# A hybrid attention and feed-forward kernel: reordered opening, paired exponentials, and a projection at another place in the first feed-forward pass

## The chip, the cores and the metric

The kernel runs on one core of one Trainium2 chip. The metric is the device time of one execution in microseconds (us). A core has five engines, each with its own queue of instructions: TensorE (PE, matrix products; its weight loads are shown apart as PEld), VectorE (DVE), ScalarE (ACT), GpSimd (POOL) and SyncE (SP, which here only issues transfers). They meet through semaphores. Each engine takes its own instructions in the order in which they were written into its queue, so an instruction that waits holds up everything behind it on its engine.

## The reference, cut to what matters

```python
x = x + attn_a(layernorm(x))   # windowed attention, 2 branches
x = x + ffn(layernorm(x))      # 4-bit weights, gelu(tanh)
x = x + attn_b(layernorm(x))   # causal attention, 16 heads, rotary
x = x + ffn(layernorm(x))      # the same weights again

# attn_a, per image, tokens of 16 channels
qkv  = tok @ qkv_w
attn = softmax(q * scale @ k.T)            # windows of 8 tokens
x1, x2 = attn @ v + depthwise_conv3x3(v)   # branch 0: rows, branch 1: columns
att  = concat(x1, x2) @ proj_w + proj_b
tok  = tok + layernorm(att) * ln_w + ln_b

# ffn
W = LUT[codes] * scales                    # gate, up (2048x256), down (256x2048)
out = (gelu(x @ Wg.T) * (x @ Wu.T)) @ Wd.T
```

`x` is 4 x 512 x 256 in f32; the four entries of the batch are called b = 0 to 3 here.

## The kernel before

**Stages.** The opening does the windowed attention of b = 0 alone, because no feed-forward work exists yet. Then come three stretches in which the feed-forward pass f0, f1, f2 of one b (`ffn`, lines 709 to 764) runs beside the window attention of the next b (`beside_window`, lines 1240 to 1260). After that the causal attentions run beside the passes f3, s0, s1, s2, and s3 ends the kernel alone.

**Order on the engines.** In the opening (lines 1158 to 1234) PE, DVE and ACT take their instructions in the order of the program text. After it only PE does (`weave`, lines 1078 to 1088). For the other engines a planner of the framework makes a fixed order at build time, by the order of the text and its own estimate of what is ready. `queue_behind` adds "not ahead of this instruction on the engine" to that.

**The weave.** The window work is a generator that yields a number of microseconds after each piece. `weave` sums these and, for each 0.86 us, puts one step of the feed-forward pass into PE's queue: one product of 512 columns or two of 256, 0.86 us of PE. A pass has 96 steps: four for the gate and up products of each of its 16 hidden blocks, and 32 for the down product, which comes in two halves after 8 blocks each. A larger yield thus puts more feed-forward products ahead of the next window piece on PE.

**The window attention.** `window_front` normalises over the group of 16 tokens: statistics, a product with `halves` (`pm`, line 249), a root on POOL (`inv_root`, lines 92 and 93), the scaling of `xa`, transposes (`yTp`), a copy `yT`, then products with the expanded weights `bw` and `taps` (`qkv`, `lepe`) whose results ACT copies into `T`. `window_consts` makes the expanded weights; it stops four times, and each `next(made)` runs it to its next stop. `window_parts` holds the pieces of the attention itself: `products` (the elementwise q times k, tile `tq`), `scores_piled` (sums on PE by products with the identity) or `scores_here` (sums on DVE), `peak` (maximum and subtraction), `power` (the exponential on ACT), `total_piled` or `total_here` (the sum of the exponentials, on PE or DVE), `shares` (the division), `weighted` (times v, tile `tv`), `values_piled` or `values_here` and `take_piled`. In the opening most sums are piled on PE; in the stretches all are on DVE. The tile `sc` of the scores has one buffer and `tmp`, which holds `tq` and `tv`, has two.

**The end of a window.** `window_back` gives four pieces: `project` (transposes `aTp`, copy, product with `pw`, then `pr` on DVE), `turn` (an inverse root and the tiles `z` on DVE), `move` (128 small products that bring `z` into the row layout, `zp`) and `add` (into `X`). `norm_rows` then makes the normalised transposed input `xT` of the feed-forward pass.

**The weights.** `dequant` expands the 4-bit weights in 12 words of six DVE instructions each, 72 items; `some(words, n)` runs n of them. Each word's two loads go to SP's queue. `along(middle, words, 6)` spends six items beside each piece of the first stretch's window and adds their yields.

**Unread products.** `busy(n)` issues n products whose result nobody reads, so that PE is not idle. All of them write one tile `idle`, which takes one of the three buffers of `fbank`; the others serve `sc`, `va`, `pg`, `pu` and `po`.

The planned lengths of the first stretch's middle:

```python
yield from between(scaled(middle, 0.87 if b == 1 else 1.22), other)
project, turn, move, add = window_back(a1, a2, wconst, b, state)
for hf in range(2):
    yield from scaled(project(hf), 0.0 if b == 1 else 1.0)
yield from turn()
```

Of the kernel before, what the change touches and what calls it, by code (L numbers as in the profile page):

```python
# [10 lines left out]
F32 = mybir.dt.float32  # L11
# [8 lines left out]
C = 16  # L20
# [15 lines left out]
def hybrid_kernel(  # L36
# [72 lines left out]
    def window_consts(aw):  # L109
        c = {}  # L110
        wrep = aw.tile([P, 48], F32, name="wrep")
        nc.gpsimd.dma_start(out=wrep, in_=qkv_w.unsqueeze(0).broadcast_to([8, C, 48]))
        prep = aw.tile([P, C], F32, name="prep")
        nc.gpsimd.dma_start(out=prep, in_=proj_w.unsqueeze(0).broadcast_to([8, C, C]))
        sh = aw.tile([P, 3, 8], F32, name="sh")
        nc.gpsimd.dma_start(out=sh, in_=shift)
        cw = aw.tile([P, 2, 3, 3, 8], F32, name="cw")
        for k, src in enumerate((conv_w0, conv_w1)):
            nc.gpsimd.dma_start(
                out=cw[:, k].rearrange("p a b c -> p (a b c)"), in_=src.broadcast_to([P, 72])  # L120
            )
        ones = aw.tile([C, P], F32, name="ones")
        nc.vector.memset(ones, 1.0)

# [114 lines left out]
    def window_front(a1, a2, c, b, y, state):  # L239
# [65 lines left out]
                    y[:, s, :], y[:, s, :], AF.Identity, bias=mean[:, s : s + 1], scale=rs[:, s : s + 1]  # L305
                )
        if b == 0:
            busy(4)
        yield 5.5 if b < 2 else 3.0

        ps = pair(f"yTp{b}")
# [29 lines left out]
        nc.scalar.copy(T[:, 7].rearrange("p s j d -> p (s j d)"), lp)  # L341
        state[b] = (y, T)

    def busy(n, cols=P):

        for _ in range(n):
            nc.tensor.matmul(idle[:, 0:cols], ident, idle_in[:, 0:cols], start=True, stop=True)

    def window_parts(a1, a2, c, b, state):

# [160 lines left out]
    def window_middle(a1, a2, c, b, state):  # L511

        w = window_parts(a1, a2, c, b, state)

        def late(br):

            behind = last_on(mybir.EngineType.Activation).name
            queue_behind(w["power"](br), behind)

        for br in range(2):  # L520
            for hf in range(2):
                ins = w["products"](br, hf)
                if br == 0:

                    queue_behind(ins, state[b - 1, "moved"] if hf == 0 else state[f"f{b - 1}"])
                w["scores_here"](br, hf)
                yield 4.6
                if br == 1 and hf == 1:
                    late(0)
            w["peak"](br)  # L530
            yield 1.4
        for br in range(2):
            w["total_here"](br)
            w["shares"](br)
            yield 2.3
            for hf in range(2):
                w["weighted"](br, hf)
                w["values_here"](br, hf)
                yield 5.1
                if br == 0 and hf == 0:  # L540
                    late(1)

    def window_back(a1, a2, c, b, state):

# [107 lines left out]
                yield 0.55  # L652


    def norm_rows(pool, b, name, out, first=4.5, at_once=False):

        xb = X[b]
        mv = pool.tile([P, 4, 2], F32, tag="mv", name=f"mv_{name}")
        def behind(ins):

            if at_once:
                queue_behind(ins, before)

        before = last_on(mybir.EngineType.DVE).name
        for i in range(4):
            st = pool.tile([P, 6], F32, tag="st", name=f"st_{name}_{i}")
            behind(nc.vector.bn_stats(st, xb[:, i, :]))
            nc.vector.bn_aggr(mv[:, i, :], st)
        rs = pool.tile([P, 4], F32, tag="rs", name=f"rs_{name}")
        inv_root(rs, mv[:, :, 1])  # L670
        xT = pool.tile([P, 2, 512], F32, tag="xT", name=f"xT_{name}", bufs=3)
        if at_once:
            yield 1.0
        before = last_on(mybir.EngineType.DVE).name
        ps = None if at_once else pair(f"xTp_{name}")
        xns = []
        for i in range(4):
            xn = pool.tile([P, 2, P], F32, tag="xn", name=f"xn_{name}_{i}", bufs=4)
            ins = nc.vector.tensor_scalar(
                xn,  # L680
                xb[:, i, :].rearrange("p (j par) -> p par j", par=2),
                mv[:, i, 0:1],
                rs[:, i : i + 1],
                ALU.subtract,
                ALU.mult,
            )
            behind(ins)
            state[name] = ins.ins.name
            xns.append(xn)
            if not at_once:  # L690
                yield first if i == 0 else 0.6
            elif i < 3:
                continue
            else:
                yield first
                ps = pair(f"xTp_{name}")
            for k in range(0 if at_once else i, i + 1):
                for par in range(2):
                    nc.tensor.transpose(ps[:, par, k * P : (k + 1) * P], xns[k][:, par, :], ident)
        nc.scalar.copy(xT, ps)  # L700
        out.append(xT)
        yield 1.3

# [437 lines left out]
    with ExitStack() as left:  # L1141
# [11 lines left out]
        idle = fbank.tile([P, 512], F32, tag="ps", name="idle")  # L1153
        idle_in = ident
        xa = window_load(a2, 0, nc.scalar)
        made = window_consts(aw)
        words = dequant(take, a1)
        with tc.manual_schedule(
            engines={mybir.EngineType.PE, mybir.EngineType.DVE, mybir.EngineType.Activation}
        ):  # L1160
            wconst = next(made)
            idle_in = wconst["sel"].rearrange("p q h n -> p (q h n)")
            front = window_front(a1, a2, wconst, 0, xa, state)
            some(front, 4)
            next(made)
            some(words, 9)
            rows_load(0)
            some(front, 3)
            ahead = window_front(a1, a2, wconst, 1, window_load(a2, 1), state)
            for b in range(1, B):  # L1170
                rows_load(b)
            drain(front)
            w = window_parts(a1, a2, wconst, 0, state)
            w["products"](0, 0)
            w["scores_piled"](0, 0)
            some(words, 3)
            next(made)
            next(ahead)
            w["products"](0, 1)
            w["scores_piled"](0, 1)  # L1180
            next(ahead)
            w["products"](1, 0)
            next(made)
            w["scores_piled"](1, 0)
            w["peak"](0)
            w["power"](0)
            next(ahead)
            w["total_piled"](0)
            w["products"](1, 1)
            w["scores_piled"](1, 1)  # L1190
            some(words, 3)
            w["shares"](0)
            w["weighted"](0, 0)
            next(ahead)
            w["values_piled"](0, 0)
            w["peak"](1)
            w["power"](1)
            w["total_piled"](1)
            w["weighted"](0, 1)
            w["values_piled"](0, 1)  # L1200
            next(ahead)
            rows_shift(wconst, 0)
            rows_shift(wconst, 1)
            some(words, 3)
            w["shares"](1)
            w["weighted"](1, 0)
            w["values_piled"](1, 0)
# [27 lines left out]

        after += [last_on(eng) for eng in (mybir.EngineType.DVE, mybir.EngineType.Activation)]
# [3 lines left out]
        def beside_window(b):  # L1240
# [136 lines left out]
```

## Time and profile before

| what | value |
|---|---|
| median of 4 runs | 1039.63 us (1038.51 to 1041.49) |
| the profiled execution: its own time | 1040.77 us |
| its span, first to last instruction | 1039.1 us |
| PE busy | 1008.8 us, 97% |
| DVE busy | 669.0 us, 64% |
| ACT busy | 357.5 us, 34% |
| POOL busy | 133.5 us, 13% |

The shares are means over stages that differ. The page of the profile also cuts the span into 40 slices of 26 us and gives the busy tenths of each engine in each. PE's busy time includes the unread products, and the ends of its products are modelled. The "granted clock" (PEclk) is the share of the full TensorE clock that the chip gave; a 0.50 means that products run at half speed.

Where the opening goes, from the instructions in order of time (us from the start of the span):

| event | start, us |
|---|---|
| first unread product (it waits for `sel` of POOL) | 6.31 |
| last statistic of b = 0 done | 7.84 |
| product `pm` | 9.71 |
| root on POOL, both instructions | 10.90 to 12.86 |
| expansion of the weights `bw` to `taps` on DVE | 14.39 to 16.67 |
| first `qkv` product | 16.72 |
| first `tq` product on DVE | 23.32 |
| `X` of b = 0 complete (`add`) | 76.08 to 77.30 |
| first product of the pass f0 | 86.56 |
| window of b = 1: `zp` | 178.46 |

### The profile page before, as it was taken

To read this page: it belongs to the slowest core of one execution; us is meant where nothing else is said; L and a number is where in the kernel's file an instruction comes from. 1 tells how busy PE (TensorE), PEld (TensorE's weight loads), DVE (VectorE), ACT (ScalarE), POOL (GpSimd) and SP (SyncE) were. 2 spreads that over 40 slices of the span, in tenths; PEclk is the share of its full clock that TensorE was granted. 3 is DMA by queue.
4 is the path that set the end of the run, shared out by engine and by line. 5 is a ranking of instruction groups with operands and counts; after the bars stand their busy time and mean duration, and the time that the engine had idled before them with its cause. 6 is when DMAs were issued, how large, how long until landed. Compare 5 with 4: busy or idle time off the path is not lost.

```text
span 1039.1 us, 13256 instructions
## 1 busy us (share of the span) xinstructions
PE 1008.8 (97%) x5058; PEld 587.2 (57%) x5058; DVE 669.0 (64%) x1579; ACT 357.5 (34%) x587; POOL 133.5 (13%) x265
## 2 busy tenths in 40 slices
PE   6999998999999999999999999999999999999998
PEld 4864545656566575564475554664644745446556
DVE  6889996956685777846586646666465576543111
ACT  2553432043213212435514435235254253451110
POOL 4100100000000012111240112310112301120000
PEclk8999999999999999999999999999999999999999
DMA  7201100000000020000000000000000000000000
GB/s 183 86 9 33 61 20 3 19 1 0 2 1 0 1 68 1 1 1 1 1 1 1 1 1 1 6 16 1 1 1 1 21 1 1 1 1 21 1 0 21
DMA packets 14031, 15.27 MB, mean 15 GB/s; under 512 B 2080, under 2 KB 10440, under 8 KB 13936
## 3 DMA queue, kind: packets, MB, share of 16 engines
q1 hardware_dynamic: 12416, 13.37, 4.3%
q10 hardware_dynamic: 1136, 0.92, 0.3%
q8 instruction: 40, 0.66, 0.3%
q0 software_dynamic: 416, 0.13, 0.2%
q14 instruction: 23, 0.19, 0.1%
HBM read 12.32 MB, written 2.10 MB: 14 GB/s over the span
## 4 chain that ended last, share of the span: by engine, by line
PE 79%; DVE 16%; issue 2%; POOL 1%; ACT 1%; POOLq 0%; DVEq 0%; ACTq 0%
PE pg_s L718 11%; PE pu_s L736 11%; PE po_s L753 10%; PE pg_f L718 7%; PE pu_f L736 7%; PE po_f L753 7%; PE s L904 4%; PE o L989 4%; PE sT L953 4%; PE qkv_b L843 3%; PE qkv L326 2%; DVE tq L398 1%; DVE tq L379 1%; DVE tq L390 1%; PE qkT L880 1%
## 5 line engine op out<-in xcount | busy, mean ns | idle before, releaser
L919 DVE CUSTOM_DVE_ANT_0 junk<-s,mask 128x512 f32<-128x512 f32 (+3 forms) x256 | 110.1, 487 | 36.8 <-PE s L904 19.8
L736 PE MATMUL pu_f<-xT_f,u 128*128 128x512 f32 x256 | 124.9, 603 | 3.0 <-ACT gs_f L730 2.0
L718 PE MATMUL pg_s<-xT_s,g 128*128 128x512 f32 x256 | 126.7, 603 | 0.0
L718 PE MATMUL pg_f<-xT_f,g 128*128 128x512 f32 x256 | 124.4, 600 | 2.2 <-ACT xT_f L700 1.1
L736 PE MATMUL pu_s<-xT_s,u 128*128 128x512 f32 x256 | 125.4, 601 | 0.0
L753 PE MATMUL po_f<-d,it_f 128*128 128x256 f32 x512 | 117.8, 381 | 1.4 <-DVE it_f L745 1.4
L753 PE MATMUL po_s<-d,it_s 128*128 128x256 f32 x512 | 118.0, 382 | 0.0
L753 PEld LDWEIGHTS po_s<-d,it_s 128*128 128x128 f32 x512 | 95.2, 190 | 20.8 <-issue 8.8
L753 PEld LDWEIGHTS po_f<-d,it_f 128*128 128x128 f32 x512 | 95.0, 190 | 19.8 <-issue 5.6
L969 POOL TENSOR_SCALAR_AFFINE_SELECT e<-e 128x256 f32<-128x256 f32 x128 | 52.7, 424 | 344.3 <-ACT e L965 341.4
L965 ACT ACTIVATE e<-sT 128x1024 f32<-128x1024 f32 (+1 forms) x72 | 66.5, 969 | 72.0 <-PE sT L953 72.0
L736 PEld LDWEIGHTS pu_f<-xT_f,u 128*128 128x128 f32 x256 | 46.9, 191 | 57.2 <-issue 49.3
L718 PEld LDWEIGHTS pg_f<-xT_f,g 128*128 128x128 f32 x256 | 46.9, 191 | 56.2 <-issue 45.6
L718 PEld LDWEIGHTS pg_s<-xT_s,g 128*128 128x128 f32 x256 | 45.9, 190 | 56.8 <-issue 50.9
L736 PEld LDWEIGHTS pu_s<-xT_s,u 128*128 128x128 f32 x256 | 46.1, 190 | 54.4 <-issue 50.2
L727 DVE SCALAR_TENSOR_TENSOR g_s<-g_s,gs_s 128x512 f32<-128x512 f32 x48 | 33.2, 691 | 58.7 <-ACT g_s L726 58.3
L730 ACT ACTIVATE gs_f<-pg_f 128x512 f32<-128x512 f32 x48 | 28.6, 596 | 93.0 <-PE pg_f L718 92.9
L745 DVE TENSOR_TENSOR it_f<-pu_f,gs_f 128x512 f32<-128x512 f32 x48 | 32.8, 683 | 32.2 <-PE pu_f L736 32.2
L724 ACT COPY gs_s<-pg_s 128x512 f32<-128x512 f32 x48 | 28.2, 587 | 67.7 <-PE pg_s L718 67.5
L904 PE MATMUL s<-kT,qT 16*128 16x384 f32 (+3 forms) x512 | 50.0, 467 | 0.0
L762 DVE TENSOR_TENSOR X<-po_s,X 128x256 f32<-128x256 f32 x32 | 13.5, 421 | 53.9 <-PE po_s L753 53.9
L989 PE MATMUL o<-e,V 128*32 128x256 f32 (+3 forms) x512 | 44.4, 441 | 0.4 <-PE sT L953 0.4
(224 smaller groups left out, 1361.7 us busy)
## 6 DMA issues: line engine op xcount, KB each, us to landing
X<-in_x_dram SPq DMA_DIRECT2D x4, 512.0 KB
out_dram<-X SPq DMA_DIRECT2D x16, 128.0 KB
xa<-in_x_dram SPq DMA_DIRECT2D x28, 64.0 KB
pkg<-in_gate_p_dram SPq DMA_DIRECT2D x4, 256.0 KB
sbg<-in_gate_s_dram SPq DMA_DIRECT2D x4, 256.0 KB
pku<-in_up_p_dram SPq DMA_DIRECT2D x4, 256.0 KB
sbu<-in_up_s_dram SPq DMA_DIRECT2D x4, 256.0 KB
pkd<-in_down_p_dram SPq DMA_DIRECT2D x4, 256.0 KB
```

What stands on the lines that cost most here:

```text
L718: nc.tensor.matmul(pg, Wf["g"][par][q][:, o : o + P], xT[:, par, :], start=par == 0, stop=par == 1)
L727: nc.vector.scalar_tensor_tensor(g2, g2, 1.0, gs, ALU.add, ALU.mult)
L736: nc.tensor.matmul(pu, Wf["u"][par][q][:, o : o + P], xT[:, par, :], start=par == 0, stop=par == 1)
L745: behind_due(nc.vector.tensor_tensor(it, pu, gs, ALU.mult))
L753: nc.tensor.matmul(po[:, 0:W], inter[k][:, i * P : (i + 1) * P], Wf["d"][par][j // 2][:, (j % 2) * W : (j % 2 + 1) * W], start=k == 0, sto ...
L843: nc.tensor.matmul(ps[:, 0, :], xT[:, par, rows], c["wqk"][:, :, par], start=par == 0, stop=par == 1)
L904: nc.tensor.matmul(pss[hl // 2][:, hl % 2, at : at + n], qT[h0 : h0 + HD, g, i * P : (i + 1) * P], kT[h0 : h0 + HD, g, 0:n], start=True, s ...
L919: nc.vector.tensor_tensor_reduce(out=junk[:, 0:n], in0=pss[k][:, hl % 2, at : at + n], in1=c["mask"][:, 512 - n : 512], scale=1.0, scalar= ...
L953: nc.tensor.matmul(pss[hl // 2][:, hl % 2, at : at + n], kT[h0 : h0 + HD + 1, g, kt * P : (kt + 1) * P], qT[h0 : h0 + HD + 1, g, kt * P : ...
L965: nc.scalar.activation(e[:, :, 0 : 512 - at0], pss[k][:, :, at0:512], AF.Exp)
L969: nc.gpsimd.affine_select(out=diag, in_=diag, pattern=[[0, 2], [1, P]], compare_op=ALU.is_ge, fill=0.0, base=0, channel_multiplier=-1,)
L989: nc.tensor.matmul(outs[g][h0 : h0 + 32, kt * P : 512], v[:, kt, 4 * g + hl, :], e[:, hl % 2, at : at + n], start=kt == 0, stop=kt == 2,)
```

## The change

The constants' loads are reordered: `conv_w0` and `conv_w1` are issued by ACT instead of POOL, and `proj_w` after them. The second part of `window_consts` (the expansion of the weights) moves ahead of the scaling of `xa`, into the time of the root. Twelve items of `words` run before the transposes of b = 0 instead of nine after them, and then fewer at each later place (2, 1, 4 and 2 instead of 3, 3, 3, 1 and 4: 21 instead of 23 by the end of the opening). All four loads of `X` are issued after the loads of `xa` for b = 1. In the opening the sums of exponentials go from PE (`total_piled`) to DVE (`total_here`), and the values of branch 0 are piled after the exponential of branch 1 is issued. Three of the four `rows_shift` run after the front of b = 1 instead of two. `busy` takes a new tile for each call and reads `ident` instead of `sel`, except at the end; its counts go from 8, 4, 2 and 10 (of 512 columns) to 8, 16, 2 and 6 (of 512). The first `norm_rows` runs two items of `words` between its root and its scaling, and its copy `xT` is split in two. In every window beside a pass both exponentials are issued after the second `peak`. For b = 1 the factor of the middle is 0.76, that of the projection 0.8 and that of the turn 1.2.

```diff
@@ window_consts
-        prep = aw.tile([P, C], F32, name="prep")
-        nc.gpsimd.dma_start(out=prep, in_=proj_w.unsqueeze(0).broadcast_to([8, C, C]))
         sh = aw.tile([P, 3, 8], F32, name="sh")
         nc.gpsimd.dma_start(out=sh, in_=shift)
         cw = aw.tile([P, 2, 3, 3, 8], F32, name="cw")
         for k, src in enumerate((conv_w0, conv_w1)):
-            nc.gpsimd.dma_start(
+            nc.scalar.dma_start(
                 out=cw[:, k].rearrange("p a b c -> p (a b c)"), in_=src.broadcast_to([P, 72])
             )
+        prep = aw.tile([P, C], F32, name="prep")
+        nc.gpsimd.dma_start(out=prep, in_=proj_w.unsqueeze(0).broadcast_to([8, C, C]))
@@ window_front
         if b == 0:
-            busy(4)
+            busy(16)
@@ busy
-    def busy(n, cols=P):
-
+    def busy(n, src=None):
+
+        ps = fbank.tile([P, 512], F32, tag="ps", name=f"idle{n}")
+        src = ident if src is None else src
         for _ in range(n):
-            nc.tensor.matmul(idle[:, 0:cols], ident, idle_in[:, 0:cols], start=True, stop=True)
+            nc.tensor.matmul(ps[:, 0 : src.shape[-1]], ident, src, start=True, stop=True)
@@ window_middle
                 w["scores_here"](br, hf)
                 yield 4.6
-                if br == 1 and hf == 1:
-                    late(0)
             w["peak"](br)
             yield 1.4
+
+        late(0)
+        late(1)
         for br in range(2):
...
                 w["values_here"](br, hf)
                 yield 5.1
-                if br == 0 and hf == 0:
-                    late(1)
@@ norm_rows
+        if aside is not None:
+            aside()
         before = last_on(mybir.EngineType.DVE).name
...
-        nc.scalar.copy(xT, ps)
+        if aside is not None:
+
+            nc.scalar.copy(xT[:, 0], ps[:, 0])
+            nc.scalar.copy(xT[:, 1], ps[:, 1])
+        else:
+            nc.scalar.copy(xT, ps)
@@ the opening
             front = window_front(a1, a2, wconst, 0, xa, state)
-            some(front, 4)
+            some(front, 2)
             next(made)
-            some(words, 9)
-            rows_load(0)
+            some(front, 2)
+            some(words, 12)
             some(front, 3)
             ahead = window_front(a1, a2, wconst, 1, window_load(a2, 1), state)
-            for b in range(1, B):
+            for b in range(B):
                 rows_load(b)
             drain(front)
             w = window_parts(a1, a2, wconst, 0, state)
             w["products"](0, 0)
             w["scores_piled"](0, 0)
-            some(words, 3)
             next(made)
             next(ahead)
             w["products"](0, 1)
             w["scores_piled"](0, 1)
             next(ahead)
             w["products"](1, 0)
-            next(made)
             w["scores_piled"](1, 0)
+            some(words, 2)
             w["peak"](0)
             w["power"](0)
             next(ahead)
-            w["total_piled"](0)
             w["products"](1, 1)
             w["scores_piled"](1, 1)
-            some(words, 3)
+            w["total_here"](0)
             w["shares"](0)
             w["weighted"](0, 0)
             next(ahead)
-            w["values_piled"](0, 0)
+            next(made)
             w["peak"](1)
             w["power"](1)
-            w["total_piled"](1)
+            w["values_piled"](0, 0)
             w["weighted"](0, 1)
             w["values_piled"](0, 1)
+            w["total_here"](1)
             next(ahead)
             rows_shift(wconst, 0)
-            rows_shift(wconst, 1)
-            some(words, 3)
             w["shares"](1)
...
-            rows_shift(wconst, 2)
-            rows_shift(wconst, 3)
+            for b in range(1, B):
+                rows_shift(wconst, b)
             some(words, 4)
             move()
             after = [last_on(mybir.EngineType.SP)]
             add()
-            busy(10, 512)
-            drain(norm_rows(f1, 0, "f0", got))
+            busy(6, wconst["sel"].rearrange("p q h n -> p (q h n)"))
+            drain(norm_rows(f1, 0, "f0", got, aside=lambda: some(words, 2)))
@@ beside_window
-            yield from between(scaled(middle, 0.87 if b == 1 else 1.22), other)
+            yield from between(scaled(middle, 0.76 if b == 1 else 1.22), other)
             project, turn, move, add = window_back(a1, a2, wconst, b, state)
             for hf in range(2):
-                yield from scaled(project(hf), 0.0 if b == 1 else 1.0)
-            yield from turn()
+                yield from scaled(project(hf), 0.8 if b == 1 else 1.0)
+            yield from scaled(turn(), 1.2 if b == 1 else 1.0)
```

More of the change, by code (lines that the diff above doesn't have):

```diff
@@ L652, in dequant, with norm_rows @@
                 yield 0.55
-    def norm_rows(pool, b, name, out, first=4.5, at_once=False):
+    def norm_rows(pool, b, name, out, first=4.5, at_once=False, aside=None):
         xb = X[b]
@@ L1151, in take @@
             return pool.tile([P, 512], dt, tag=tag, name=name)
-        idle = fbank.tile([P, 512], F32, tag="ps", name="idle")
-        idle_in = ident
         xa = window_load(a2, 0, nc.scalar)
@@ L1161, in hybrid_kernel @@
             wconst = next(made)
-            idle_in = wconst["sel"].rearrange("p q h n -> p (q h n)")
             front = window_front(a1, a2, wconst, 0, xa, state)
-            some(front, 4)
+            some(front, 2)
             next(made)
-            some(words, 9)
-            rows_load(0)
+            some(front, 2)
+            some(words, 12)
             some(front, 3)
             ahead = window_front(a1, a2, wconst, 1, window_load(a2, 1), state)
-            for b in range(1, B):
+            for b in range(B):
                 rows_load(b)
```

## The prediction

> **What bounds the kernel now.** I read the page's 40 busy slices of 26 us first (tenths busy), then busy time by stretch.
>
> ```profile
> PE   6999998999999999999999999999999999999998
> DVE  6889996956685777846586646666465576543111
> ```
>
> PE is short only in the first slice and in the seventh (156 to 182 us); DVE is nearly full only in the first seven.
>
> ```profile
> 72.00:177.00 105.00, 97.58 (x416) 53.57 (x414) 94.26 (x153) 40.55 (x86) 4.02 (x5) 0.98 0.10 31
> 177.00:275.00 98.00, 96.07 (x449) 59.96 (x450) 69.02 (x114) 26.39 (x39) 3.04 (x4) 1.00 0.02 6
> 392.00:560.00 168.00, 167.23 (x889) 92.70 (x888) 110.88 (x318) 68.07 (x103) 37.02 (x74) 1.00 0.00 1
> ```
>
> Columns: stretch and length, then busy us of PE, PEld, DVE, ACT, POOL, then granted clock. From 177 us on PE is the bound: it lacks 1.9 us of 98, later 0.8 of 168, so whatever is won earlier reaches the end. In the first stretch beside a pass DVE is full as well: 94.26 of 105. The change touches two places: the opening, where PE has no pass to run, and this DVE-full stretch. For the opening I read the chain of waits up to 80 us (start, length, what):
>
> ```profile
> 6.31 3.56 PE idle L347 x16
> 9.87 0.14 PE pm L249 x2
> ...
> 14.47 0.65 DVE bw L168 x2
> ...
> 44.81 3.72 PE va L374 x16
> 48.53 1.75 PE sm L374 x16
> ...
> 80.97 1.39 DVE xn_f L679 x4
> 82.35 2.20 DVE tq L390
> ```
>
> The chain passes through unread products (6.31), and the piled sum `sm` stands between two DVE pieces. The list of instructions in order of time gives the rest (start, length, engine, line; in brackets idle time before and its releaser):
>
> ```profile
> 7.66 0.18 DVE L278 BATCH_NORM_AGGREGATE mva<-sta 128x2 f32<-128x6 f32 x1
> 75.73 8.85 PE L347 MATMUL idle<-sel,ident 128*128 128x512 f32 x20
> 84.42 1.04 PE L699 MATMUL xTp_f<-ident,xn_f 128*128 128x128 f32 x8
> 86.56 1.98 PE L718 MATMUL pg_f<-xT_f,g 128*128 128x512 f32 x4 [1.10 <-ACT xT_f L700]
> 135.35 3.38 PE L736 MATMUL pu_f<-xT_f,u 128*128 128x512 f32 x4 [2.02 <-ACT gs_f L730]
> 164.47 0.60 PE L556 MATMUL aTp<-ident,att 128*128 128x128 f32 x4
> 178.46 3.70 PE L598 MATMUL zp<-z,sel 128*32 128x128 f32 x128 [2.37 <-DVE z L580]
> 157.73 0.42 DVE L487 TENSOR_TENSOR att<-tv,T 128x256 f32<-128x256 f32 x1
> 167.01 0.69 DVE L565 TENSOR_TENSOR pr<-aTp,pb 128x512 f32<-128x512 f32 x1 [7.59 <-PE aTp L562]
> ```
>
> The statistics end at 7.84, but `pm` starts at 9.71 behind the unread products; the transposes of `xn` (ready 81.4 to 82.4) stand behind them until 84.42. In the first stretch DVE has `att` of half 0 at 158.1, PE reaches the projection at 164.47, DVE idles 7.59 us, and then PE waits 2.37 for `z`.
>
> **Opening, first part.** The first unread products need only `ident` (POOL, done 2.66): they run 2.7 to 6.3, and `pm` starts at 7.9 instead of 9.71: -1.8. The root ends at 11.05. The expansion (14.39 to 16.67, 2.29 long) goes into the root's wait from 9.0 to 11.3, 0.25 over it, so the last `xa` is done at 12.85 instead of 14.47 (-1.6). If `cw`, now issued by ACT behind four loads (3.71), takes the 5.2 us to land that it took from POOL, it arrives near 10 against a need at 9.7: 0 to 0.9 late; I take 0. ACT's extra two issues (0.65 each, the row of its `xa` loads) are hidden before its first work at 13.10. Twelve items at 3.58 a word (16.58 to 20.16) keep DVE until 20.0. Their loads are there: `pkg`, `pku` and `sbu` released the later `xa` issues on SP by 15.91. Moving the load of X for b = 0 behind eight `xa` issues costs nothing while X is first read at 51.47.
>
> T must be ready too. From the first `qkv` (16.72) to `tq` (23.32) it took 6.6, part at granted clock 0.50 (13 to 19.4 us); at the later spacing of 2.15 a pair it is 4.95. Sixteen unread products before the transposes are 32 passes at 0.1425 (9.85 to 10.99) or 0.2225 (6.31 to 9.87): they end at 12.6 or 15.2. Fast: transposes end 13.1, the copy (1.01) 14.2, T 19.1, so `tq` starts at 20.0. Slow throughout: 24.8. PE is busy in nearly all of 2.7 to 13, so I take 20.7, near the fast end: -2.6.
>
> **Opening, attention.** By DVE and PE rows (tq 2.21, pile 3.6, reduce plus subtract 1.4, reduce of `total_here` 1.05 as in the later window, reciprocal and product 1.3, tv 2.30) I walk the new text: `tq` 20.7, second 24.8, third 27.3 (its buffer waits for the first pile), two items to 30.6, peak 30.9, fourth 32.3, total 34.5, first `tv` 36.9, peak 39.4, second 41.0, total 43.4, `tv` 45.7, its pile 48.0 to 51.7. From `tq` to here 31.0 against 34.5 (23.32 to 57.82): -3.5. It comes from seven items fewer (9 to 2, some 4 us of DVE) and from `sm` (1.75 of PE plus its wait, twice) against 1.05 on DVE. Up to `zp` nothing changes. The four items then are cheaper kinds (2.1 against 2.5): X is added at 69.7 instead of 76.08, -6.4. The later `rows_shift` is 12 x 0.41 = 4.9 us of ACT from 66.5, done by 71.4, hidden until the copy of `xT` at 76.4; uncovered, the four extra cost 1.65.
>
> **Towards f0.** Add to last `xn` took 6.27. Two items of 0.72 in the root's wait (idle 1.42): +0.03. Window b = 1 starts its `tq` at 76.0 (82.35 before, -6.35). Twelve unread passes of 0.43 end near 74.9, ahead of the last `xn`; transpose 0.3 and half a copy (0.59) put the first `pg` at 77.05, -9.5.
>
> **First stretch.** DVE does not gain those 9.5 but 6.35. From `tq` to `att` of half 0 it worked without a gap, 82.35 to 158.07 = 75.7. After: three more items (+0.94), and two hidden blocks fewer are due before it (2 x 0.6): 75.45, so 151.45. PE comes sooner: the yields before the projection were (46.2 + 23.75) x 0.87 = 60.9 and are (46.2 + 24.7) x 0.76 = 53.9; with 9.8 of front products and some 2 of waits PE stands at the projection from 142.7. It waits 8.7 us, where it was late before. From the projection to `zp`: DVE 1.9 + 1.2 + 11.3 = 14.4; PE, by its yields (0.96 + 1.44 twice, 8.64) and its own products, 16.4, so `z` is no wait and `zp` is at 167.85: -10.6. Steps given out before `zp` fall from 68.0 to 67.3: 0.7 back, -9.9. Hidden here: the feed-forward steps left after `zp` (82.6 - 67.3 = 15.3) cover add and norm as they did (14.6); if not, `xT` is next.
>
> The 8.7 us wait has a clock price. The row at 135.35 shows it: after a 2.02 us wait `pu` took 3.38 instead of 1.72, with 0.83 granted in that 10 us, that is 3.4 us at half speed: 1.7 lost. The opening's 9.5 to 12.9 agrees: 1.5 us of products, then 0.50. I charge 1.7; the bounds are 0 (the wait splits into small ones) and 3.4 (twice). The loss at 135 itself was hidden in DVE's time, so I count no gain for it.
>
> [...]
>
> **Exponentials.** Four table loads (1.28) a window could become two, but `sc` has one buffer: branch 1's scores can't be written before exponential 0, which now queues behind the front's last ACT piece (`off`, `yT`). In b = 1 it moves from 27.9 us after `tq` to about 33; DVE has items to fill this: 0, or 5 if the fixed order stands there. In b = 2 and 3 some 6 us later, under slack of 10 (`att` 253.5, projection 264): 0. So they are "together" only with sums and a peak (2.3 us) between; I count 0.
>
> **Sum.** -9.9 + 1.7 = -8.2: span 1039.1 to 1030.9, its own time 1040.77 to 1032.6. That execution lies 1.1 over the median, so against the median 1031.4.
>
> **Rivals.** (a) Forecast, 1031.4, own range 1028 to 1035: 0.62. (b) The opening's clock stays low: T at 24.8, +4.1, and a second cold window, +1.7: 1037.2, no change. For: 13 to 19.4 at 0.50. Against: products nearly everywhere from 2.7 on. 0.12. (c) PE bounds the first stretch, because the planner lets the items slip behind `att`: 9.5 of the opening and most of the 9.7 us that PE lost there (2.0 + 2.02 + 1.7 + 1.4 + 2.37, rounded): about 1024. Against: DVE 94.26 of 105, and the items are needed by `pg` and `po`. 0.17. (d) Slower: DVE stands in its fixed order before the sums of branch 1 until exponential 0. Its front waits for PE, and PE for `it` behind the standing DVE. Each us moves `att`; from 11.3 us on (8.2 plus 0.3%) the kernel is slower, and with 14 it ends at 1045. For: one buffer. Against: DVE had no idle entry on ACT in 82 to 159. 0.09. That the exponentials don't pair at all changes (a) by under 1.3.
>
> **Numbers.** About 0.3% (3.1 us) can be told from no change here. Faster (under 1036.5): a, c and a quarter of b: 0.82. Same 0.10 (most of b, a little of d). Slower 0.08. The range, 1026 to 1037, holds a, half of c and half of b.
>
> **What would show it.** `pm` near 7.9; `tq` at 20 to 21; no `sm` on PE; X added near 70; first `pg` near 77; DVE without gaps to about 151; PE waiting for `att` at line 556 for some 9 us; `zp` near 168 with no wait; clock under 1 after the projection. Wrong if `tq` comes after 23, if DVE idles on an exponential in the first stretch, or if PE reaches the projection after `att`.

## The result and the profile after

The changed kernel takes 1040.04 us (median of 37 runs, 1037.71 to 1044.47) against 1039.08 us for the kernel before (59 runs on the same chips, 1038.46 to 1043.24): a ratio of 1.0007, 95% interval 1.0000 to 1.0013. No difference can be told. 1031.4 was forecast.

The profiled execution has a span of 1037.9 us (own time 1039.59) against 1039.1 before. Its busy slices (tenths busy, 40 slices of 26 us) and its busy time by stretch, with the columns explained above:

```profile
PE   7988789999999999999999999999999999999998
DVE  7989996848675877846586655666465575543111
```

```profile
72.00:177.00 105.00, 92.75 (x373) 50.92 (x375) 95.75 (x152) 33.69 (x77) 4.58 (x5) 0.95 0.10 30
177.00:275.00 98.00, 96.32 (x368) 58.47 (x357) 66.46 (x119) 24.42 (x38) 3.04 (x4) 1.00 0.02 5
```

From 72 to 177 us PE works 4.8 us less than before (92.75 against 97.58) and at a mean granted clock of 0.95 instead of 0.98, beside a DVE that is as full as before. The chain of waits up to 80 us (start, length, what) shows that the opening did what the prediction said:

```profile
8.45 0.40 PE pm L249 x2
8.85 5.29 PE idle L349 x32
14.14 0.89 PE yTp L313 x8
...
48.46 3.72 PE va L376 x16
...
70.23 1.23 DVE X L610
...
74.43 1.46 POOL rs_f L93
75.92 1.38 DVE xn_f L682 x4
77.30 2.20 DVE tq L392
```

`sm` is gone, `pm` starts 1.3 us sooner, X is added at 70.23 (76.08 before), window 1 starts at 77.3 (82.3), and the first `pg` at 78.47 (86.56): 8.1 us won. The list of PE's instructions shows where they go (start, length; in brackets idle time before and its releaser):

```profile
78.47 1.98 PE L726 MATMUL pg_f<-xT_f,g 128*128 128x512 f32 x4 [0.67 <-ACT xT_f L705]
...
92.06 1.98 PE L744 MATMUL pu_f<-xT_f,u 128*128 128x512 f32 x4 [1.31 <-DVE it_f L753]
...
105.54 1.98 PE L744 MATMUL pu_f<-xT_f,u 128*128 128x512 f32 x4 [2.69 <-DVE it_f L753]
...
113.15 3.78 PE L744 MATMUL pu_f<-xT_f,u 128*128 128x512 f32 x4 [3.92 <-DVE it_f L753]
...
134.45 2.85 PE L726 MATMUL pg_f<-xT_f,g 128*128 128x512 f32 x4 [2.71 <-DVE X L770]
...
158.41 0.60 PE L557 MATMUL aTp<-ident,att 128*128 128x128 f32 x4
174.32 3.70 PE L599 MATMUL zp<-z,sel 128*32 128x128 f32 x128
```

PE waits four times for a buffer of `fbank`, because DVE has not yet multiplied a hidden block (`it_f`) or added a sum (X). After two of the waits its products run slow (3.78 us for what takes 1.88; granted clock 0.66 from 110 to 120 us, 0.83 from 130 to 140). All of PE's waits for hidden blocks and for X from 77 to 190 us, before and after (total, times, longest):

```profile
PE po_f L753 <- DVE it_f L745: 1.4, 2, 0.9
PE pu_f L736 <- DVE it_f L745: 0.6, 1, 0.6
```

```profile
PE pu_f L744 <- DVE it_f L753: 7.9, 3, 3.9
PE pg_f L726 <- DVE X L770: 2.7, 1, 2.7
PE po_f L761 <- DVE it_f L753: 1.3, 1, 1.3
```

PE reaches the projection 6.1 us sooner than before and `zp` 4.1 us sooner; by the last transposes ahead of the second pass 2.6 are left, at the fourth window 1.1, and 1.2 at the end.

DVE's list shows why the blocks are late: the pieces of window 1 and of the expansion stand between them. First the changed kernel, with blocks 3, 4 and 5, then the kernel before, with blocks 4 and 5:

```profile
97.18 0.69 DVE L753 TENSOR_TENSOR it_f<-pu_f,gs_f 128x512 f32<-128x512 f32 x1
97.78 0.69 DVE L639 SCALAR_TENSOR_TENSOR dwg<-pkg,dwg 128x512 int32<-128x512 int32 x1
98.38 2.29 DVE L400 TENSOR_TENSOR tq<-T 128x2048 f32<-128x2048 f32 x1
...
104.79 0.69 DVE L753 TENSOR_TENSOR it_f<-pu_f,gs_f 128x512 f32<-128x512 f32 x1
105.39 0.69 DVE L639 SCALAR_TENSOR_TENSOR dwu<-pku,dwu 128x512 int32<-128x512 int32 x1
105.99 2.29 DVE L400 TENSOR_TENSOR tq<-T 128x2048 f32<-128x2048 f32 x1
...
112.41 0.69 DVE L753 TENSOR_TENSOR it_f<-pu_f,gs_f 128x512 f32<-128x512 f32 x1
```

```profile
109.51 0.68 DVE L745 TENSOR_TENSOR it_f<-pu_f,gs_f 128x512 f32<-128x512 f32 x1
110.11 0.68 DVE L641 SCALAR_TENSOR_TENSOR pku<-dwu 128x512 int32<-128x512 int32 x1
110.71 0.68 DVE L745 TENSOR_TENSOR it_f<-pu_f,gs_f 128x512 f32<-128x512 f32 x1
111.31 0.41 DVE L381 TENSOR_TENSOR sc<-tq 128x256 f32<-128x256 f32 x1
111.98 2.28 DVE L398 TENSOR_TENSOR tq<-T 128x2048 f32<-128x2048 f32 x1
```

In the changed kernel 7.6 us pass from one hidden block to the next, twice, and a `tq` stands between blocks 4 and 5 that stood behind both before. PE needs one every 3.44 us (its two products of 1.72). No entry of DVE between 94 and 121 us has idle time before it: DVE does not wait, it does other things first. Start of the eight hidden blocks of the first half, counted from window 1's first `tq` on DVE:

| kernel | first `pg` | blocks 0 to 7 (us after the first `tq`) |
|---|---|---|
| before | 4.3 | 10.7, 15.4, 16.6, 21.2, 27.2, 28.4, 36.1, 37.3 |
| changed | 1.2 | 6.2, 14.1, 15.3, 20.0, 27.6, 35.2, 36.4, 40.2 |

Two things add up: PE comes 3.1 us sooner relative to DVE, and block 5 stands 6.8 us later in DVE's order. The longest wait is for it: PE's product at 113.15 takes the buffer that block 5 gives back. Before, the same product (113.78) came 2.4 us after block 5 was done and did not wait for it. Without its three waits PE would have been there at 28.0 us after the first `tq`; block 5 is done at 35.9, and the three waits at `pu` are the 7.9 us between.

A sum over the twelve 10 us windows from 70 to 190 us, PE's idle time and the time lost by the granted clock (10 us times what it lacks to 1), makes a rough account: before 8.9 + 1.7 = 10.6 us, after 13.6 + 5.1 = 18.7. Of the idle time 1.1 and 1.6 us lie ahead of the first `pg`; from it on 9.5 us are lost before and 17.1 after. The difference, 7.6 us, is most of the 8.1 us won at the first `pg`.

### The profile page after: what moved, and what is told of

Read it like the earlier page. It is cut to its first block, busy times and chain, and to the rows that moved or that the text cites. A ratio compares the mean times of both kernels' runs of the same rounds, so it can differ in the third digit from the quotient of the medians.

```text
span 1037.9 us, 13219 instructions
## 1 busy us (share of the span) xinstructions
PE 1005.9 (97%) x5042; PEld 585.2 (56%) x5042; DVE 671.7 (65%) x1581; ACT 349.5 (34%) x582; POOL 134.3 (13%) x263
## 4 chain that ended last, share of the span: by engine, by line
PE 80%; DVE 15%; issue 1%; ACT 1%; POOL 1%; DMA 1%; SPq 0%; POOLq 0%; DVEq 0%; ACTq 0%
PE pg_s L726 11%; PE pu_s L744 11%; PE po_s L761 11%; PE pg_f L726 8%; PE pu_f L744 8%; PE po_f L761 6%; PE s L912 5%; PE o L997 4%; PE sT L961 4%; PE qkv_b L851 3%; PE qkv L326 2%; DVE tq L381 2%; DVE tq L400 1%; PE qkT L888 1%; PE qkv_b L855 1%; DVE tv L467 1%
```

## The experiments

Three theories were set against each other, and each expectation below was written before its run. W: DVE's full first stretch and the half clock spend the gain. S: the new factors spend it. P: the paired exponentials spend it. After the first four runs W was split in two: L (DVE has too much to do) and O (its fixed order has the window's pieces ahead of the hidden blocks). "Idle" and "half clock" below are the two sums from 70 to 190 us of the run's profile; times are medians, ratios are to the kernel before on the same chip.

**The opening alone** (the changed kernel with the old exponentials and factors):

```diff
-        late(0)
-        late(1)
+                if br == 1 and hf == 1:
+                    late(0)
...
+                if br == 0 and hf == 0:
+                    late(1)
...
-            yield from between(scaled(middle, 0.76 if b == 1 else 1.22), other)
+            yield from between(scaled(middle, 0.87 if b == 1 else 1.22), other)
-                yield from scaled(project(hf), 0.8 if b == 1 else 1.0)
-            yield from scaled(turn(), 1.2 if b == 1 else 1.0)
+                yield from scaled(project(hf), 0.0 if b == 1 else 1.0)
+            yield from turn()
```

> The opening's edits alone; the exponentials and the three factors of the first stretch as before. Theory W (the first stretch is full on DVE, so the opening is worth only what DVE starts earlier, 5.1 us, less what PE loses by waiting and by a low clock): 3 to 5 us faster than before, first gate product near 78.5, waits of PE for hidden blocks between 2 and 6 us. Rival S (the new factors spend the gain): 5 to 8 us faster. Rival P (the paired exponentials spend it): also 5 to 8 us faster; the other runs tell S from P.

Measured 1038.38, ratio 0.9996 (0.9985 to 1.0006): no theory has its number, since W too forecast 3 us or more. First `pg` 81.09, idle 11.9, half clock 6.8; the profiled execution is the slowest of the twelve (1041.22). In it the first pass starts 5.5 us sooner and PE is at the projection at 164.70, before 164.47: all of it is lost between. So neither the pair nor the factors are needed to lose it, and S and P cannot be the whole.

**The pair alone, and the factors alone**, on the kernel before (the same lines, the other way):

> Before with only the two exponentials issued after the second peak. Theory W: within 1.5 us of before, since DVE has words to do while the scores' one buffer is held; table loads in the three stretches fall. Rival P: 2 to 4 us slower, with hidden blocks of the first stretch later on DVE.

Measured 1042.03, ratio 1.0027 (1.0015 to 1.0040): P's number, not W's. P's mechanism is not seen in the first stretch, where blocks 5 and 7 stand at 28.5 and 36.1 us (28.4 and 37.3 before); PE waits 2.1 us for X instead.

> Before with only the factors 0.76, 0.8 and 1.2. Theory W: PE reaches the projection 7 us sooner, where DVE has its input at 158 as before; PE gains at most the 7.6 us that DVE idled, less waits: within 3 us of before either way. Rival S: 2 to 4 us slower, because fewer steps of the pass are handed out beside the same DVE work, so hidden blocks stand later in DVE's order and PE waits for them, with granted clock under 1 in 100 to 140 us.

Measured 1041.05, ratio 1.0018 (1.0009 to 1.0027), at the lower end of S and within W. S's mechanism is seen: block 5 stands at 34.9 us instead of 28.4, and the granted clock is 0.83 from 110 to 120 us. Both cost something where the opening is old.

**The changed kernel with the old factors**:

> The changed kernel with the factors back at 0.87, 0 and 1. Theory W: within 2 us of the changed kernel (1040), because DVE's work up to the projection's input is the same. Rival S: 3 to 6 us faster than the changed kernel, that is 1034 to 1037, with under 4 us of waits for hidden blocks. Rival P: like the changed kernel.

Measured 1040.88, ratio 1.0011 (1.0001 to 1.0021), idle 13.7, half clock 1.7: W's number, not S's. The factors are not what keeps the changed kernel from its gain.

**Less work on DVE** (L against O): half of the expansion left out.

```diff
-        for at, n in enumerate(("g0", "u0", "g1", "u1", "d0", "d1", "g2", "u2", "g3", "u3", "d2", "d3")):
+        for at, n in enumerate(("g0", "u0", "g1", "u1", "d0", "d1")):
...
-                        pg, Wf["g"][par][q][:, o : o + P], xT[:, par, :], start=par == 0, stop=par == 1
+                        pg, Wf["g"][par][q % 2][:, o : o + P], xT[:, par, :], start=par == 0, stop=par == 1
```

(and the same for u and d; the result is not the reference's).

> The changed kernel with half of the weight expansion left out: only the first six of the twelve pieces (g0, u0, g1, u1, d0, d1) are expanded, and the feed-forward uses these two quarters of each matrix for all four, so its output is not the reference's. Some 36 DVE items, about 20 us of DVE time beside window 1, are gone; DVE's order is the planner's own. Theory L (load: the gain is lost because DVE has too much to do in the first stretch): PE's waits for hidden blocks (7.9 + 1.3 us) and X (2.7) go, no half clock is left: median 1029 to 1033. Theory O (order: the window's pieces stand ahead of the hidden blocks in DVE's fixed order, at whatever load): adding row durations along DVE's order from window 1's first tq, the hidden blocks still stand at 6, 14, 15, 22, 28, 29, 33 and 43 us (the changed kernel: 6, 14, 15, 20, 28, 35, 36, 40; PE could use them from about 8 on, every 3.4 us), so the eighth is 12 us late as before; PE is idle some 14 us between the first pg and 190, with half clock after the waits: median 1036 to 1041.

Measured 1040.77, ratio 1.0013 (1.0002 to 1.0024), idle 13.9, half clock 5.1. DVE is free from 140 to 150 us (0.85 of 10 us busy), and PE waits as long as ever. Its waits by releaser, 70 to 190 us (total, times, longest):

```profile
PE po_f L761 <- DVE it_f L753: 6.4, 2, 6.1
PE pu_f L744 <- DVE it_f L753: 4.6, 3, 2.9
```

The eighth block starts 44.9 us after the first `tq`, later than in the changed kernel (40.2). L falls: DVE's busy time is 17.6 us less than in the changed kernel (654.1 for 671.7), `att` of half 0 is complete 19.4 us sooner after the first `tq` (57.2 for 76.6), and nothing is gained. What less work would be worth with the blocks in time is not shown.

**Another order, nothing left out**:

```diff
+    def shaped(work, first, n, rest):
+        for k, w in enumerate(work):
+            yield w * (first if k < n else rest)
...
-                middle = along(middle, words, 6)
+                middle = along(middle, words, 3)
...
-            yield from between(scaled(middle, 0.76 if b == 1 else 1.22), other)
+            yield from between(shaped(middle, 1.0, 6, 0.8) if b == 1 else scaled(middle, 1.22), other)
```

> The changed kernel with nothing left out; only the order beside window 1 is altered: three items of the expansion with each piece of the window instead of six, and the pieces' factor 1.0 for the first six and 0.8 for the rest instead of 0.76, so that more PE steps, and with them more hidden blocks, come between two pieces. By DVE's order of the built kernel the hidden blocks of the first half stand at 6, 12, 13, 17, 23, 23, 29, 30 us after window 1's first tq instead of 6, 14, 15, 20, 28, 35, 36, 40. DVE's work is the same. Theory L: nothing gained, 1039 to 1041. Theory O: PE's idle time from the first pg to 190 falls from 13.6 us to 5 to 8, the half clock from 5.1 to at most 1.7: median 1029 to 1034, faster than both kernels.

Measured 1031.70, ratio 0.9923 (0.9910 to 0.9935); first `pg` 78.64, idle 7.6, half clock 1.7. The blocks stand at 5.8, 12.2, 12.8, 16.6, 22.6, 23.2, 29.3 and 30.3 us. PE's instructions around the place where it had waited, and all its waits from 77 to 190 us:

```profile
104.71 1.88 PE L744 MATMUL pu_f<-xT_f,u 128*128 128x512 f32 x4
106.43 1.89 PE L761 MATMUL po_f<-d,it_f 128*128 128x256 f32 x8
108.16 0.28 PE L249 MATMUL pm<-mva,halves 128*128 128x8 f32 x2
108.30 12.33 PE L761 MATMUL po_f<-d,it_f 128*128 128x256 f32 x56
122.36 1.98 PE L726 MATMUL pg_f<-xT_f,g 128*128 128x512 f32 x4 [1.73 <-DVE X L770]
```

```profile
PE pu_f L744 <- DVE u L650: 1.8, 1, 1.8
PE pg_f L726 <- DVE X L770: 1.7, 1, 1.7
PE xTp_f L702 <- DVE xn_f L682: 1.3, 1, 1.3
PE pg_f L726 <- ACT xT_f L708: 1.1, 1, 1.1
PE pg_f L726 <- ACT xT_f L705: 0.7, 1, 0.7
```

No wait for `it_f` is left in the whole first pass. The same work on DVE, in another order, is 8.3 us faster than the changed kernel. O holds. `att` of half 0 is also complete sooner, 62.9 us after the first `tq` for 76.6, since the expansion is spread further; that this alone is no cure the run with three items and the old factor shows below.

**The same order with the old opening**:

> The same order edit on the kernel before with its old opening (it has the paired exponentials and the new factors too): it differs from the kernel with the altered order by the opening alone. Theory O: where the hidden blocks are not late, the opening's 8 us arrive in full, so this one is 8 to 10 us slower than the altered order with the new opening: 1037 to 1042. If the opening's gain is lost for another reason that the order does not cure, the two are within 4 us of each other.

Measured 1039.85, ratio 1.0004 (0.9995 to 1.0013). With the hidden blocks in time the opening is worth 1039.85 - 1031.70 = 8.2 us, where the two first `pg` lie 7.3 us apart (85.92 and 78.64). Behind the old opening the altered order brings nothing over the kernel before (1039.85 against 1039.08): it pays only together with the earlier start.

**The fourth cell, the old opening under the given order**, with pair and factors:

> The kernel before with the paired exponentials and the new factors: the changed kernel with the old opening and its order of expansion, six items with each piece. It is the fourth cell of opening (old, new) by order (given, altered); the other three are 1040.0 (new, given), 1039.9 (old, altered), 1031.7 (new, altered). Theory O: under the given order the opening is worth about nothing, 1039 to 1042. If the pair and the factors alone spend the gain of the opening (alone they cost 2.8 and 1.9 us), they spend it here too: 1043 to 1046.

Measured 1044.84, ratio 1.0057 (1.0044 to 1.0070): O's number is missed, the other side's is met. Its list of PE's instructions:

```profile
115.95 3.42 PE L735 MATMUL pu_f<-xT_f,u 128*128 128x512 f32 x4 [3.31 <-DVE it_f L744]
137.88 2.93 PE L717 MATMUL pg_f<-xT_f,g 128*128 128x512 f32 x3 [4.47 <-DVE X L761]
```

The mechanism is the same here, a hidden block and a sum that stand too late on DVE, but it is the pair and the factors that put them there (block 5 at 34.3 us, before 28.4; with the factors alone 34.9). So the table of six:

| median us | old opening | new opening | the opening is worth |
|---|---|---|---|
| old exponentials and factors, six items | 1039.1 | 1038.4 | 0.7 |
| pair and new factors, six items | 1044.8 | 1040.0 | 4.8 |
| pair, three items, factors 1.0 and 0.8 | 1039.9 | 1031.7 | 8.2 |

The rows come from different chips; by the ratios the opening is worth 0.4, 5.2 and 8.4, and the first cannot be told from nothing. The change is its opening, whose worth depends on the order that follows, and a rest that costs 5.8 on the old opening and 1.7 on the new. They are not two separate effects that happen to cancel: both make PE meet the same late hidden blocks, so what one costs or gains depends on the other.

**One half of the order at a time**: three items with the factor 0.76, and six items with the factors 1.0 and 0.8.

> One half of the altered order: the changed kernel with three items with each piece, and its factor 0.76. DVE's order has the hidden blocks at 6, 12, 16, 22, 28, 33, 36, 43 and X's last sum at 60: still some 12 us behind what PE could use. Theory O: PE idle 11 to 14 us with half clock, 1036 to 1040. If three items were the cure by themselves: 1030 to 1034.

Measured 1038.71, ratio 0.9994 (0.9981 to 1.0008), O's number; idle 10.4, half clock 3.4. `att` of half 0 is complete at 62.5 us, as early as in the altered order, but the eighth block stands at 44.8.

> The other half: the changed kernel with six items and the factors 1.0 and 0.8. Hidden blocks at 6, 10, 15, 16, 21, 28, 29, 36, X's sums at 38 to 50, att complete at 78. Theory O: half of the lateness gone, PE idle 9 to 11 us: 1034 to 1038. If the factors were the cure by themselves: 1030 to 1033.

Measured 1040.78, ratio 1.0018 (1.0003 to 1.0032), a miss for both: idle 11.3, half clock 3.4, and 2.7 and 3.4 more from 190 to 290. Its two longest entries of waits from 70 to 300 us:

```profile
PE xTp_f L702 <- DVE xn_f L682: 5.2, 2, 4.3
PE po_f L761 <- DVE it_f L753: 3.2, 1, 3.2
```

Hidden blocks that are asked for sooner push the end of window 1 back when six items come with each piece: a good part of the wait moves to `xn`, and with 14.0 us PE's idle time from 70 to 290 is near the changed kernel's 14.6. Of these three orders only both halves together leave no wait of over 2 us.

**Unread products where PE waits** (the half clock by itself):

```diff
+                if name == "f0" and n in {4: 8, 6: 16, 7: 24}:
+                    fl = one(f"fill{n}")
+                    for _ in range({4: 8, 6: 16, 7: 24}[n]):
+                        nc.tensor.matmul(fl[:, 0:P], ident, ident, start=True, stop=True)
                 for par in range(2):
```

> The changed kernel with 8, 16 and 24 unread 128-column products ahead of the up products of hidden blocks 4, 6 and 7 of the first pass, where PE waited 1.3, 2.7 and 3.9 us. DVE's order stays the same up to the eighth hidden block (it stands 1.6 us later there). They fill waits and cost at most 1 to 2 us where a wait is shorter. Clock theory (half clock in 110 to 120 costs 3.4 us by itself): granted clock 1.0 there, median 1036 to 1039. If the half clock is hidden behind DVE's order, so that PE would wait anyway: 1040 to 1042.

Measured 1039.53, ratio 0.9999 (0.9988 to 1.0009). In its profile the clock is 1.00 from 110 to 120 us, and `zp` starts at 176.48, 2.2 later than without. The median lies between the two expectations and says little. The run does not separate the clock from the rest: the unread products took longer than the waits that they fill (the `pu` of block 7 starts 3.2 us later, at 116.34), the eighth block stands at 42.1 instead of 40.2, and from 130 to 140 us the clock is 0.72 instead of 0.83. That the half clock from 110 to 120 us had been hidden is only argued: PE waits for the sum X afterwards in both, 2.71 us until 134.45 in the changed kernel and 3.29 until 135.55 here.

**A late `att` as a rival to O** (five items, factors 1.2 and 0.6, exponentials apart):

> Another order, exponentials apart: five items with each piece, factors 1.2 for the first six pieces and 0.6 for the rest. Hidden blocks at 6, 10, 15, 15, 21, 23, 26 and 30 us after the first tq, X's four sums done by 44 (51 in the altered order, 63 in the changed kernel), att complete at 78 instead of 69. Theory O: PE idle 6 to 8 us from the first pg to 190 and no or one half clock, 1028 to 1032. Theory L, by which late att would cost: 1035 or more.

Measured 1036.02, ratio 0.9963 (0.9951 to 0.9975), a miss for O's number; the other side's, 1035 or more, is met. No wait for `it_f` is left, but 3.4 us in one piece for `xn`, the end of the window whose `att` is late (77.7 us), and 4.0 for ACT's `gs`, with 5.1 of half clock up to 200 us. Blocks in time are not sufficient; what DVE is made to do later must not be late in its turn. Why `gs` is late was not tested.

**The pair under the good order**, twice, and fewer unread products in the opening:

> The altered order (three items with each piece, factors 1.0 and 0.8) with the exponentials apart as before, one behind each branch's peak and the other behind the first values: it differs from the altered order by the pair alone. If the pair has a price of its own (alone on the kernel before it cost 2.8 us, 1.0027), this one is 2 to 3 us faster: 1028 to 1030. If that price too was only a shift of the hidden blocks in DVE's order (theory O), the two are within 1.5 us: 1030 to 1033. By DVE's order the eighth hidden block stands at 33 us after the first tq, against 30 with the pair.

> The altered order with the exponentials apart, unchanged, for comparison on the same chip: 1029 to 1031. A second set of runs for the pair's price: with the pair the altered order took 1031.7.

Measured 1029.84 and 1030.27, ratios 0.9911 (0.9895 to 0.9927) and 0.9917 (0.9901 to 0.9933), against 0.9923 (0.9910 to 0.9935) with the pair. The intervals overlap, so these times do not settle what the pair costs there (1.9 and 1.4 us by the medians). A part of it stands in the profiles: in the third stretch, from 290 to 400 us, `pg` waits 1.3 us for X in each of the ten profiled executions with the pair, and 0.3 in each of the seven without it. So 1.0 us is the pair's whatever the opening and the order, and it is most of what the changed kernel loses between the second pass and the fourth window (2.6 to 1.1).

```diff
         if b == 0:
-            busy(16)
+            busy(8)
```

> The altered order with the exponentials apart, and 8 unread products in place of 16 ahead of the first transposes of window 0. In the changed kernel's profile the 16 took 5.45 us and the transposes started as they ended, at 13.98, with the last xa at 13.9. If they hold the transposes back: up to 2 us faster than the same kernel with 16 (1029.8). If they only fill a wait for xa, or keep the clock up for the qkv products: the same within 1 us, or slower by up to 4 us where the first pairs run at half clock.

Measured 1028.12, ratio 0.9901 (0.9886 to 0.9917). The lowest median of all, but by less than its interval. In its profile the transposes wait 0.65 for `xa` and no longer for the unread products.

Kernels that are faster than both: the altered order, 1031.7; the same with the exponentials apart, 1029.8 and 1030.3; and this with 8 unread products, 1028.1.

## Why the prediction was wrong, step by step

- **Opening: right, 0.5 late.** `pm` 8.45 for 7.9, since a load of `xa` landed late (DVE waited 0.91 us for it, 0.33 before) and the statistics ended at 8.41. The expansion waited 0.62 for `cw`, inside the bounds 0 to 0.9 of which 0 was taken. The unread products ended at 14.1, between 12.6 and 15.2, nearer the slow end, and the transposes stood behind them. `tq` 21.24 for 20.7, the last pile 48.46 to 52.18 for 48.0 to 51.7, X 70.23 for 69.7.
- **Towards f0: 1.4 short.** 0.5 of it is X above; the root on POOL took 2.1 us (73.8 to 75.9) for 1.3 before. So window 1's `tq` came at 77.3 for 76.0 and the first `pg` at 78.47 for 77.05.
- **DVE's stretch: right as a total.** `att` of half 0 is complete 76.6 us after `tq`; 75.45 was said.
- **The step that failed:** "with 9.8 of front products and some 2 of waits PE stands at the projection from 142.7. It waits 8.7 us". PE stood there at 158.41 and did not wait. Of the 15.7 us, about 15.1 are the 1.4 above, 10.6 of waits for hidden blocks and X where 2 were counted, and 5.1 of half clock. Even the losses before were more than 2: rival (c) lists 2.0, 2.02 and 1.7 of them ahead of the projection, 5.7 in all. (Its five terms add up to 9.5, not 9.7.) DVE's full stretch was taken as one total that ends with `att`. But the hidden blocks are part of it, each has its own due time, and PE cannot pass one. The rows shown before had the numbers: PE was put 9.5 us forward and DVE 6.35, so every block that PE met without slack (it waited 0.6 and 1.4 for them before) had to be 3.1 us late. That block 5 would also stand 6.8 us later in DVE's order was in no row of the kernel before. The order experiment (1031.7 with the same DVE work) shows that it is the order, and the relief (1040.8 with `att` 19.4 us sooner) that less work is no cure while the blocks are late.
- **The new factors** were counted as "PE comes sooner" to the projection. With a smaller factor fewer PE steps, and so fewer hidden blocks, come between two pieces of the window: with the old factors and the rest of the change blocks 5 and 7 stand at 28.8 and 37.0 us, with the new ones at 35.2 and 40.2. Alone on the kernel before the factors cost 1.9, together with the pair 5.8.
- **Clock charge 1.7, bounds 0 to 3.4:** 5.1 in the profile, and elsewhere. The wait that was to cause it did not exist.
- **Exponentials 0:** rival (d)'s mechanism was not seen; DVE idled 0.19 us on one in the first stretch. Alone on the kernel before, the pair cost 2.8. In the third stretch, where 0 was counted under a slack of 10 us at the projection, PE waits 1.0 us longer for X: the same step again, a sum with a due time of its own inside a stretch that was read by its end.
- **"z is no wait":** right, but since PE was late, not since DVE was early.
- **The sum** counted the opening's gain at `zp` in full (-9.9); 4.1 arrived there. The rivals had a low clock in the opening, a bound on PE and a standing DVE; that PE would be held by hidden blocks in DVE's order without any wait of DVE was among none of them.
- **The slices** were read loosely: PE's last slice is an 8 as well, and DVE's first and seventh are 6 while its eighth is 9. No term hung on this.

## What to carry to other kernels

Where two engines run in fixed orders and one is full, put down for both how far each moves: if the consumer comes forward more than the producer, the difference appears as a wait at the first product without slack, however early the last one is. A factor that only spaces one engine's work also sets where its products stand in the other's order, so retune it after every change of the part before. And before an earlier start is given up as worthless, measure it again under another order: here the same opening was worth 0.7 (not to be told from nothing), 4.8 and 8.2 us.

## What the hardware showed that was not expected

The same opening gave the first `pg` at 76.72 to 82.14 us in ten profiled executions, a range of 5.4 us; the old one at 85.26 to 87.94 in five. Two rows vary in these ten: `pm` starts at 7.63 to 10.34, when the statistics of `xa` are done (in the changed kernel's profile they wait 0.91 us for a load of `xa`), and the same 16 unread products take 3.82 to 6.66 us (5.45 in the changed kernel's profile). In the execution where they took 6.44 the granted clock was 1.00 all the while, as in the one with 3.82, so the granted clock alone does not tell the speed of products in the first 20 us.

In the 17 profiles the clock lost from 70 to 190 us comes to 0, 1.7, 3.4, 5.1 or 6.8 us, that is in units of 1.7: 3.4 us at half speed (in the kernel before the granted clock is 0.50 from 135.8 to 139.2 us). Each unit lies in or behind a wait of 1.6 us or more (the longest 6.1), but not each such wait has one. The wait of 2.0 us at `gs` cost a unit in the kernel before and in the opening alone; with the pair alone and with the old factors the same wait, followed by another of 2.1, cost nothing (1.00 from 130 to 140 us), and neither did 2.4 us at `zp` before. With the altered order and the exponentials apart, the wait of a `pu` for `u` cost a unit at 1.63 us in the run with 8 unread products (0.84 from 130 to 140 us) and none at 1.64 us in the two with 16 (1.00). So the row that the prediction read, 2.02 us and half clock, is one of two outcomes. Why equal waits cost a unit or none was not shown. The runs of one kernel lie up to some 7 us apart (1037.71 to 1044.47 in the changed kernel).
